# Attention scores from fp32r halves in place of float32 products, and cross-attention queries over 512 columns, in a two-layer decoder

## The chip, the cores and the metric

The kernel runs on one core of a Trainium2 chip. The metric is the device time of one launch, in microseconds (us); less is better. A second record, the trace, holds every instruction of one execution, and the profile is a page made from it. The engines are called PE (TensorE's matmuls), PEld (TensorE's loads of the stationary matrix), DVE (VectorE), ACT (ScalarE), POOL (GpSimd) and SP (the engine whose queue issues the DMAs here).

## The reference

The input x has 16 batches of 64 tokens of width 512, and a context of the same shape. Six blocks follow one another; after each, x becomes the layer norm of x plus the block's output.

```python
x = _layernorm(x + _L0_attn_ref(...))    # causal GQA, 32 query heads, 8 kv heads, width 128
x = _layernorm(x + _L0_xattn_ref(...))   # linear attention over channels, 8 heads of 64
x = _layernorm(x + _L0_ffn_ref(...))     # int4 weights with group scales, inner width 1792
x = _layernorm(x + _L1_attn_ref(...))    # causal GQA with an ALiBi bias on sqrt(distance)
x = _layernorm(x + _L1_xattn_ref(...))   # GQA on the context, queries and keys over their rms
x = _layernorm(x + _L1_ffn_ref(...))     # dense base plus gated low-rank experts
```

The three attentions with 32 heads share one shape: for each batch and kv head, four query heads of 64 queries meet 64 keys.

```python
scores = einsum(q, k) / sqrt(128) + bias     # bias: causal mask, ALiBi, or the given mask
out = softmax(scores) @ v @ w_o
```

All is float32.

## The kernel before

A float32 matrix is used on TensorE as two fp32r matrices: hi, the value rounded to fp32r, and lo, the rest. `mm3` (L101) computes a product as hi*hi + hi*lo + lo*hi, three matmuls into one PSUM bank. `split_sb` and `split_ps` make the halves: ScalarE copies hi, then GpSimd (from SBUF) or VectorE (from PSUM) subtracts. A few small products go to TensorE as plain float32; the trace records each of these as two matmuls. Among them are the scores.

**Tiling.** There are eight token tiles of 128 (two batches each) and two halves of 512 tokens. `Attn` (L737) is one attention layer. For L0 and L1, `q_unit` makes the queries of one query head for half of the tokens, transposed, into `qt` [128, 8 batches, 256], and `k_unit` the keys into `kt`; both copy from a bank of tag `mm` on ScalarE. For the cross attention, `qn_front` (L790) makes the queries of a token tile, token-major, in a bank `fx` as two halves of 256 columns, and divides them by their rms (`rms`); `qn_back` (L803) transposes them into `qt`. The keys of the context are made early by `kv_stream` (L165) and go through DRAM (`ktd`), the values too (`xvd`).

**The stream.** `Stream.run` (L970) goes through steps; a step is four batches of one kv head, and a layer has 32. Within a step, projections for two steps later, the transposes of the probabilities (`pt`, L874), the output projection of the step before (`oproj`, L897), the product with V (`av`, L884) and the scores of two steps later (`scores`, L847) follow one another. `scores` makes eight products of [128 (two heads' queries)] x [64 keys] into the one bank `sc`, then runs the softmax: scale and mask, maximum, subtraction, exponent, sum, division, and the split into `p`, hi and lo side by side.

**What runs beside it.** `fill` puts pieces of other blocks between the parts of a step. Beside the first half of L0's attention runs `k_stream` (L271), the linear attention's key side; beside the second half `q_stream(0)` (L359), its query side in five stages with lags in ticks. Then `l0_ffn` (L440) runs beside `q_stream(1)` and `kv_stream`. L1's attention and the cross attention are one stream, and the last ffn's steps are filled in at its end.

**What sets the order.** The code's order gives priorities; a planner places the instructions on each engine's queue before the run, and may let a ready one pass one that waits for a buffer. Each engine takes its queue in order. Buffers are rings by tag:

```python
BUFS = {"st": 6, "wq": 6, "wo": 6, "wk": 2, "wv": 2, "v": 4, "vs": 4, "qt": 2, "kt": 2, "s": 3, "p": 3, "pts": 2, "ot": 4}
BANKS = {"mm": 2, "fx": 3, "sc": 1, "pt": 1, "o": 1}
```

All eight PSUM banks are used. `fx` serves `k_stream`, `q_stream`, `qn_front`, `qn_back`, and parts of the L0 ffn, whose partial products go through the banks of `PART_BANKS` in turn. `st` holds the loads from DRAM before they are split; `v` holds the halves of V on their way to DRAM (`store_v`, L147).

Of the kernel before, what the change touches and what calls it, by code (L numbers as in the profile page):

```python
# [21 lines left out]
B, S, D = 16, 64, 512          # batches, tokens of a batch, model width  # L22
NT = B * S // 128              # token tiles of 128 (two batches each)
KV, G, HD = 8, 4, 128          # kv heads, query heads of each, head width
FF = 1792 // 128               # tiles of the L0 ffn's inner width
NEG = -1.0e30

# A float32 matrix x is used on the tensor engine as hi + lo, two fp32r
# matrices: hi = x rounded to fp32r, lo = x - hi, which is exact.  A product is
# hi*hi + hi*lo + lo*hi in float32 accumulation.  # L30


# Tiles in SBUF by tag: how many, each of the size of the first use.
BUFS = {"st": 6, "wq": 6, "wo": 6, "wk": 2, "wv": 2, "v": 4, "vs": 4, "qt": 2, "kt": 2, "s": 3, "p": 3, "pts": 2, "ot": 4}
BANKS = {"mm": 2, "fx": 3, "sc": 1, "pt": 1, "o": 1}
# The banks that the partial products of the L0 ffn and its down products go through in turn.
PART_BANKS, DOWN_BANKS = ("o", "sc", "fx", "fx", "fx"), ("o", "sc")
# L0 ffn tiles (14 for each half of the tokens) from this one on go with integer weights.
INT_FROM = 6
# The order in which the L1 ffn's steps of the last four token tiles are taken, by step of the stream and fill point.  # L40
# [7 lines left out]
class Net:  # L48
    def __init__(self, ctx, tc, a):
# [14 lines left out]
        # x by token tile; x transposed, hi and lo, by half of the tokens: [d, dk, token]  # L64
# [9 lines left out]
    def soon(self):  # L74
        """The softmax and what feeds its products goes before the projections' own evacuations."""
        return self.tc.high_priority(offset=100)
# [7 lines left out]
    def split_sb(self, src, hi, lo, fast=False):  # L84
        """hi, lo from float32 in SBUF."""
        self.nc.scalar.copy(hi, src)  # L86
        (self.nc.vector if fast else self.nc.gpsimd).tensor_tensor(lo, src, hi.bitcast(F32), ALU.subtract)  # L87

    def split_ps(self, src, hi, lo):
        """hi, lo from float32 in PSUM."""  # L90
        self.nc.scalar.copy(hi, src)  # L91
        self.nc.vector.tensor_tensor(lo, src, hi.bitcast(F32), ALU.subtract)  # L92

    def load_split(self, src, hi, lo, fast=False):
        """DRAM [128, n <= 1024] -> hi, lo in SBUF."""
# [5 lines left out]
    def mm3(self, out, pairs, first=True, last=True):  # L101
        """out (+)= sum over pairs (lh, ll, rh, rl) of lh*rh + lh*rl + ll*rh."""
# [6 lines left out]
    def rpow(self, out, v, eps, scale=1.0):  # L109
        """out = (v * scale + eps) ** -0.5"""  # L110
# [36 lines left out]
    def store_v(self, vd, t, col, ps):  # L147
        """V [128 tokens, 256] of a token tile -> hi, lo in DRAM, columns col.."""
# [5 lines left out]
    def rms(self, src, dst):  # L154
        """dst [128, n, 128] = src (PSUM) over its rms along the last axis; the last step is returned."""
# [9 lines left out]
    def kv_stream(self):  # L165
        """K (normalized, transposed) and V of the context, to DRAM; a unit of work at a time."""
        nc, a = self.nc, self.a
        self.ktd = self.dram.tile([KV, HD, B * S], F32, name="ktd")
# [12 lines left out]
        def back(hp, t, kn):  # L181
            pk = self.bank("pt")[:, 0:256].rearrange("p (h t) -> p h t", h=2)
            for i in range(2):
                nc.tensor.transpose(pk[:, i], kn[:, i], self.ident)
            ks = self.t("pts", [128, 2, 128])
            nc.scalar.activation(ks, pk, AF.Copy, scale=w)
            nc.sync.dma_start(self.ktd[2 * hp:2 * hp + 2, :, t * 128:(t + 1) * 128].rearrange("h d t -> d h t"), ks)
# [38 lines left out]
    def load_dup(self, src):  # L226
        """src [64, 512] on both halves of the partitions."""
# [5 lines left out]
    def lin_setup(self, ctx):  # L233
# [5 lines left out]
        # WW[c, h, o] = sum over e of Wv[h, e, c] Wout[o, h, e] less its mean over o, on both halves  # L239
# [23 lines left out]
    def half_split(self, src, half):  # L263
        """[64, 512] on the partitions of a half -> hi and lo stacked on 128."""
# [6 lines left out]
    def k_stream(self):  # L271
        """The keys' side: M[b][hd, o] = (softmax(K) V^T Wout^T) / 8, less its mean over o, to DRAM.

        An item is two of the four 128 rows hd of a batch; its four stages are spread over the ticks."""
# [5 lines left out]
        def logits(i):  # L280
# [11 lines left out]
            # exp of the logits [hd, n] less their maximum; the sum divides later  # L292
# [66 lines left out]
    def q_stream(self, half):  # L359
        """The queries' side, the residual, LN and transposition of x; a chunk of 128 n at a time, in stages."""  # L360
# [4 lines left out]
        self.split_sb(self.load_dup(self.a["wq_lin"]), *wq)  # L365

        def logits(c):
# [10 lines left out]
            s = live[c] = self.t(("s", "p")[c % 2], [128, 8, 64])  # L378
# [15 lines left out]
        def transpose(c):  # L394
# [4 lines left out]
            qh = qhs[c] = ex.tile([128, 4, 128], F32, name="le", bufs=3)  # L399
            nc.scalar.copy(flat(qh), pt)  # L400

        def out(c):
# [9 lines left out]
            if u == 1 and k == 3:  # L412
                # over the deviation along o
                z2 = ex.tile([128, 8, 64], F32, name="le", bufs=3)
# [15 lines left out]
        stages = ((5, out), (4, transpose), (2, norm), (1, exp), (0, logits))  # L430
# [9 lines left out]
    def l0_ffn(self, final):  # L440
        """Half after half of the tokens; a unit of work at a time.

        A tile of the inner width is an item.  Either its gate and up weights are multiplied by their scales
        (hi, lo), or the integers go to the tensor engine as they are, which takes two products rather than
        three, and the sum over the groups of a scaled product is left to the vector engine.  An int4 weight is
        exact in fp32r, as is any integer of up to 11 bits: its lo is zero."""
# [4 lines left out]
        def dequant(q, s, hi, lo):  # L451
            """q [128, 1024] ints times s (the same on all partitions) -> hi, lo."""
# [40 lines left out]
        for n, (half, it, ints) in enumerate(items):  # L493
# [3 lines left out]
            if i == 0:  # L497
                pair = self.t("qt", [128, 2, 2, 512], FR)
            # silu(gate) * up, with sigmoid(gate) = (1 + tanh(gate / 2)) / 2
# [27 lines left out]
            self.split_sb(sg, pair[:, 0, i], pair[:, 1, i])  # L527
# [6 lines left out]
            if i == 1:  # L534
                if pend:
                    dn = load_down(g)
                pend = (half, g, dn, pair[:, 0], pair[:, 1])
# [5 lines left out]
    def l1_ffn_setup(self, cp):  # L543
        """The weights; a load at a time."""
# [23 lines left out]
    def l1_ffn(self, t, end):  # L568
        """A token tile: gate, base, experts with residual, LN, out; three steps.  At the end the stream's banks are free."""
# [9 lines left out]
        # threshold: 0.125 / (1 + exp(-(z + b)))  # L579
# [36 lines left out]
    def run(self):  # L616
# [5 lines left out]
        NS = 4 * KV                                  # steps of a layer  # L622
# [11 lines left out]
        with ExitStack() as ctx:  # L634
            # L0: attention; the linear attention's keys beside its first half, its queries a half later
# [460 lines left out]
```

## Time and profile before

| | us |
|---|---|
| three runs | 2274.55, 2277.70, 2279.82 |
| median of the runs | 2277.70 |
| profiled execution, first to last instruction (its span) | 2275.4 |
| PE busy | 2208.5 |
| PEld busy | 1917.7 |
| DVE busy | 1346.0 |
| POOL busy | 1172.9 |
| ACT busy | 1124.1 |

The profiled execution has no other time of its own than the span; the median of the runs is 2.3 us above it. The granted TensorE clock is 0.994 of full speed. The stages by window: L0's attention up to some 690 us, the L0 ffn with the rest of the linear attention and the context's keys and values up to some 1150, L1's attention to some 1700, the cross attention and the last ffn to the end.

A line of the groups by line and shape reads: line, engine, operation, output <- inputs (partitions x elements), count | busy us, mean ns of one | idle time before them. A line of the timeline reads: start, us from the start of the first to the end of the last of the merged instructions, engine, line, operation, tiles, shape, count.

### The profile page before, as it was taken

To read this page: it belongs to the slowest core of one execution; us is meant where nothing else is said; L and a number is where in the kernel's file an instruction comes from. 1 tells how busy PE (TensorE), PEld (TensorE's weight loads), DVE (VectorE), ACT (ScalarE), POOL (GpSimd) and SP (SyncE) were. 2 spreads that over 40 slices of the span, in tenths; PEclk is the share of its full clock that TensorE was granted. 3 is DMA by queue.
4 is the path that set the end of the run, shared out by engine and by line. 5 is a ranking of instruction groups with operands and counts; after the bars stand their busy time and mean duration, and the time that the engine had idled before them with its cause. 6 is when DMAs were issued, how large, how long until landed. Compare 5 with 4: busy or idle time off the path is not lost.

```text
span 2275.4 us, 36680 instructions
## 1 busy us (share of the span) xinstructions
PE 2208.5 (97%) x13200; PEld 1917.7 (84%) x13200; DVE 1346.0 (59%) x2523; ACT 1124.1 (49%) x2195; POOL 1172.9 (52%) x1001
## 2 busy tenths in 40 slices
PE   8999999999999999999999999999999999999998
PEld 7888888888888777777788888888898899988996
DVE  3655555667645789887743343433356566666656
ACT  5665556555444455555444444444444454443442
POOL 3533334455554655464654554545455666554641
PEclk9999999999999999999999999999999999999999
DMA  7533333322334322456543443334333343332320
GB/s 231 158 115 109 112 105 120 110 84 77 91 114 154 120 83 86 153 180 184 156 144 106 131 126 119 116 111 140 107 113 101 115 123 99 103 105 85 112 70 29
DMA packets 255317, 267.24 MB, mean 117 GB/s; under 512 B 32672, under 2 KB 168352, under 8 KB 255136
## 3 DMA queue, kind: packets, MB, share of 16 engines
q1 hardware_dynamic: 255136, 264.90, 38.1%
q8 instruction: 105, 1.72, 0.3%
q14 instruction: 76, 0.62, 0.1%
HBM read 231.26 MB, written 33.55 MB: 116 GB/s over the span
## 4 chain that ended last, share of the span: by engine, by line
PE 79%; DMA 5%; DVE 5%; POOL 5%; issue 2%; ACT 2%; SPq 0%; POOLq 0%; DVEq 0%; ACTq 0%
PE mm L105 16%; PE mm L106 15%; PE mm L107 15%; PE sc L856 6%; PE o L889 4%; PE fx L105 3%; PE fx L107 3%; PE fx L106 3%; PE pt L878 2%; DMA st<-in_down_s 1%; POOL wo L87 1%; PE fx L325 1%; POOL wq L87 1%; PE fx L298 1%; PE fx L316 1%
## 5 line engine op out<-in xcount | busy, mean ns | idle before, releaser
L87 POOL TENSOR_TENSOR wq<-st,wq 128x512 fp32r<-128x512 f32 x200 | 263.7, 1331 | 329.2 <-ACT wq L86 326.1
L107 PE MATMUL mm<-wo,ot 128*128 128x512 f32 x896 | 352.2, 393 | 0.0
L87 POOL TENSOR_TENSOR wo<-st,wo 128x512 fp32r<-128x512 f32 x226 | 296.6, 1342 | 96.8 <-ACT wo L86 88.0
L105 PE MATMUL mm<-wo,ot 128*128 128x512 f32 x768 | 315.2, 410 | 3.4 <-DVE x L904 3.1
L904 DVE TENSOR_TENSOR x<-x,mm 128x512 f32<-128x512 f32 x192 | 131.1, 683 | 308.2 <-PE mm L107 307.8
L106 PE MATMUL mm<-wo,ot 128*128 128x512 f32 x768 | 301.1, 392 | 0.0
L105 PE MATMUL mm<-xth,wq 128*128 128x512 f32 x512 | 204.9, 400 | 0.6 <-DVE v L92 0.3
L106 PE MATMUL mm<-xtl,wq 128*128 128x512 f32 x512 | 200.9, 392 | 0.0
L107 PE MATMUL mm<-xth,wq 128*128 128x512 f32 x512 | 200.6, 392 | 0.0
L107 PEld LDWEIGHTS mm<-wo,ot 128*128 128x128 f32 x896 | 169.3, 189 | 37.1
L91 ACT CAST ot<-o 128x512 fp32r<-128x512 f32 x192 | 112.3, 585 | 174.6 <-PE o L889 173.6
L114 POOL TENSOR_TENSOR r<-e,nhalf 128x4 f32<-128x4 f32 (+1 forms) x96 | 88.6, 923 | 203.2 <-DVE e L113 194.2
L86 ACT CAST wq<-st 128x512 fp32r<-128x512 f32 x204 | 123.8, 620 | 130.7 <-PE mm L106 73.5
L856 PEld LDWEIGHTS sc<-kt,qt 128*128 128x128 f32 x1536 | 184.4, 193 | 3.1
L856 PE MATMUL sc<-kt,qt 128*128 128x64 f32 x1536 | 185.0, 273 | 0.0
L92 DVE TENSOR_TENSOR ot<-o,ot 128x512 fp32r<-128x512 f32 x192 | 132.0, 687 | 81.8 <-ACT ot L91 81.5
L870 POOL TENSOR_TENSOR s<-s,rc 128x512 f32<-128x512 f32 x96 | 100.6, 1048 | 141.7 <-DVE rc L869 77.4
L105 PEld LDWEIGHTS mm<-wo,ot 128*128 128x128 f32 x768 | 144.6, 188 | 27.9 <-DVE x L904 3.4
L106 PEld LDWEIGHTS mm<-wo,ot 128*128 128x128 f32 x768 | 145.3, 189 | 24.1
L86 ACT CAST wo<-st 128x512 fp32r<-128x512 f32 x226 | 129.7, 624 | 41.0 <-PE mm L106 21.9
L105 PE MATMUL fx<-wq,xth 128*128 128x256 f32 x512 | 149.3, 292 | 0.0
L107 PE MATMUL fx<-wq,xtl 128*128 128x256 f32 x512 | 145.5, 284 | 0.0
(283 smaller groups left out, 5626.1 us busy)
## 6 DMA issues: line engine op xcount, KB each, us to landing
st<-in_wq SPq DMA_DIRECT2D x128, 256.0 KB, 3.1
st<-in_wo SPq DMA_DIRECT2D x128, 256.0 KB, 3.1
vs<-v SPq DMA_DIRECT2D x256, 128.0 KB, 3.1
v<-v SPq DMA_DIRECT2D x128, 128.0 KB, 2.7
st<-in_wqx SPq DMA_DIRECT2D x64, 256.0 KB, 2.9
st<-in_wox SPq DMA_DIRECT2D x64, 256.0 KB, 3.4
vs<-xv SPq DMA_DIRECT2D x128, 128.0 KB, 3.0
st<-in_gu_q SPq DMA_DIRECT2D x56, 256.0 KB, 3.0
```

Source lines behind the costliest of these rows:

```text
L86: self.nc.scalar.copy(hi, src)
L87: (self.nc.vector if fast else self.nc.gpsimd).tensor_tensor(lo, src, hi.bitcast(F32), ALU.subtract)
L91: self.nc.scalar.copy(hi, src)
L92: self.nc.vector.tensor_tensor(lo, src, hi.bitcast(F32), ALU.subtract)
L105: self.nc.tensor.matmul(out, lh, rh, start=first and i == 0, stop=False)
L106: self.nc.tensor.matmul(out, lh, rl, start=False, stop=False)
L107: self.nc.tensor.matmul(out, ll, rh, start=False, stop=last and i == n - 1)
L114: self.nc.gpsimd.tensor_tensor(out, e, self.nhalf[:, :n], ALU.pow)
L856: nc.tensor.matmul(sc[:, i * 64:(i + 1) * 64], qt[:, c + b, gp * 128:(gp + 1) * 128], kt[:, (c + b) * 64:(c + b + 1) * 64], start=True, st ...
L870: nc.gpsimd.tensor_tensor(x, x, rc.unsqueeze(2).to_broadcast([128, 8, 64]), ALU.mult)
L889: nc.tensor.matmul(o[:, b * 256:(b + 1) * 256], self.vs[s][i][:, bp * 2 + b], pts[:, b * 256:(b + 1) * 256], start=i == 0, stop=i == 1)
L904: self.nc.vector.tensor_tensor(n.x[t], n.x[t], ps, ALU.add)
```

## The change

The queries and keys of all three attentions are kept as fp32r hi and lo. The keys' halves lie side by side, so that a block of scores is two products: hi of the queries with hi and lo of the keys (128 columns), and lo of the queries with hi of the keys (64 columns, added to the first). The eight blocks of a step now fill two banks, and the softmax's first operation is done in four parts. The evacuations of queries and keys become splits, the context's keys go through DRAM as pairs. Cross queries take their weights by rows of the input instead of by columns, so that a product is 512 columns wide. To make room, `fx` has two banks, several rings are shorter, the query tiles are six small ones, and `q_stream` keeps its intermediate tiles in a ring of its own. All comments are removed, which is left out here.

```diff
-BUFS = {"st": 6, "wq": 6, "wo": 6, "wk": 2, "wv": 2, "v": 4, "vs": 4, "qt": 2, "kt": 2, "s": 3, "p": 3, "pts": 2, "ot": 4}
-BANKS = {"mm": 2, "fx": 3, "sc": 1, "pt": 1, "o": 1}
-PART_BANKS, DOWN_BANKS = ("o", "sc", "fx", "fx", "fx"), ("o", "sc")
+BUFS = {"st": 5, "wq": 6, "wo": 6, "wk": 2, "wv": 2, "v": 2, "vs": 4, "qt": 6, "kt": 2, "s": 3, "p": 2, "pts": 2, "ot": 3}
+BANKS = {"mm": 2, "fx": 2, "sc": 2, "pt": 1, "o": 1}
+PART_BANKS, DOWN_BANKS = ("o", "sc", "sc", "fx", "fx"), ("o", "sc")
...
     def kv_stream(self):
-        self.ktd = self.dram.tile([KV, HD, B * S], F32, name="ktd")
+        self.ktd = self.dram.tile([KV, HD, B, 2 * S], F32, name="ktd")
...
-            ks = self.t("pts", [128, 2, 128])
-            nc.scalar.activation(ks, pk, AF.Copy, scale=w)
-            nc.sync.dma_start(self.ktd[2 * hp:2 * hp + 2, :, t * 128:(t + 1) * 128].rearrange("h d t -> d h t"), ks)
+            ks = self.t("pts", [128, 4, 128], FR)
+            pb = pk.rearrange("p h (b t) -> p (h b) t", b=2)
+            nc.scalar.activation(ks[:, :, 0:64], pb, AF.Copy, scale=w)
+            nc.vector.scalar_tensor_tensor(ks[:, :, 64:128], pb, w, ks[:, :, 0:64].bitcast(F32), ALU.mult, ALU.subtract)
+            for i in range(2):
+                nc.sync.dma_start(self.ktd[2 * hp + i, :, 2 * t:2 * t + 2], ks[:, 2 * i:2 * i + 2].bitcast(F32))
...
     def q_stream(self, half):
+        ring = [ex.tile([128, 2, 512], F32, name="le", bufs=3) for _ in range(3)]
...
-            s = live[c] = self.t(("s", "p")[c % 2], [128, 8, 64])
+            s = live[c] = ring[c // 2 % 2][:, c % 2].rearrange("p (h d) -> p h d", h=8)
...
-            qh = qhs[c] = ex.tile([128, 4, 128], F32, name="le", bufs=3)
+            qh = qhs[c] = ring[2][:, c % 2].rearrange("p (j n) -> p j n", j=4)
...
-                z2 = ex.tile([128, 8, 64], F32, name="le", bufs=3)
+                z2 = self.t("s", [128, 8, 64])
...
-        stages = ((5, out), (4, transpose), (2, norm), (1, exp), (0, logits))
+        stages = ((4, out), (3, transpose), (2, norm), (1, exp), (0, logits))
...
     def l0_ffn(self, final):
-                pair = self.t("qt", [128, 2, 2, 512], FR)
+                pair = [self.t("qt", [128, 2, 512], FR) for _ in range(2)]
...
     def k_unit(self, half, h):
-        kt = self.kt[half, h] = n.t("kt", [128, 512])
+        kt = self.kt[half, h] = n.t("kt", [128, 8, 128], FR)
...
-        self.nc.scalar.copy(kt, ps)
+        n.split_ps(ps.rearrange("p (b t) -> p b t", b=8), kt[:, :, 0:64], kt[:, :, 64:128])
+
+    def q_tiles(self, half, h):
+        self.qt[half, h] = [[self.n.t("qt", [128, 4, 256], FR) for _ in range(2)] for _ in range(2)]
...
     def q_unit(self, half, h, g):
-        self.nc.scalar.copy(self.qt[half, h][:, :, g * 64:(g + 1) * 64], ps.rearrange("p (b q) -> p b q", b=8))
+        for q, qt in enumerate(self.qt[half, h]):
+            n.split_ps(ps[:, q * 256:(q + 1) * 256].rearrange("p (b q) -> p b q", b=4),
+                       *[t[:, :, g * 64:(g + 1) * 64] for t in qt])
...
     def qn_front(self, half, h, i):
-        for gp in range(2):
-            w = self.wqs[h, gp]
-            n.mm3(ps[:, gp * 256:(gp + 1) * 256], [n.xt_slices(t, k) + (w[0][:, k], w[1][:, k]) for k in range(4)])
+        ws = [[flat(w).rearrange("p (k c) -> p k c", k=2) for w in self.wqs[h, kp]] for kp in range(2)]
+        n.mm3(ps, [n.xt_slices(t, k) + (ws[k // 2][0][:, k % 2], ws[k // 2][1][:, k % 2]) for k in range(4)])
...
     def qn_back(self, half, h, i):
-        dst = self.qt[half, h][:, 2 * i:2 * i + 2].rearrange("p b (g q) -> p b g q", g=4)
-        self.nc.scalar.copy(dst, ps.rearrange("p g (b q) -> p b g q", b=2))
+        r = slice(2 * (i % 2), 2 * (i % 2) + 2)
+        n.split_ps(ps.rearrange("p g (b q) -> p b g q", b=2),
+                   *[t[:, r].rearrange("p b (g q) -> p b g q", g=4) for t in self.qt[half, h][i // 2]])
...
     def scores(self, s):
-        qt, kt, c = at.qt[half, h], at.kt[half, h], (s % 2) * 4
-        sc = n.bank("sc")
-        for b in range(4):
-            for gp in range(2):
-                i = b * 2 + gp
-                nc.tensor.matmul(sc[:, i * 64:(i + 1) * 64], qt[:, c + b, gp * 128:(gp + 1) * 128],
-                                 kt[:, (c + b) * 64:(c + b + 1) * 64], start=True, stop=True)
-        m, d = (at.mask, (8, 64)) if at.alibi is None else (at.alibi[:, h], (4, 128))
+        (qh, ql), kt, c = at.qt[half, h][s % 2], at.kt[half, h], (s % 2) * 4
+        sc = [n.bank("sc").rearrange("p (u i k) -> p u i k", u=2, i=4) for _ in range(2)]
+        for i in range(8):
+            o, b, q = sc[i // 4][:, :, i % 4], i // 2, slice((i % 2) * 128, (i % 2) * 128 + 128)
+            nc.tensor.matmul(o, qh[:, b, q], kt[:, c + b].rearrange("p (u k) -> p u k", u=2), start=True, stop=False)
+            nc.tensor.matmul(o[:, 0], ql[:, b, q], kt[:, c + b, 0:64], start=False, stop=True)
+        m, d = (at.mask, (4, 64)) if at.alibi is None else (at.alibi[:, h], (2, 128))
...
-            nc.vector.scalar_tensor_tensor(flat(x).rearrange("p (a b) -> p a b", b=d[1]),
-                                           sc.rearrange("p (a b) -> p a b", b=d[1]), 1.0 / math.sqrt(HD),
-                                           m.unsqueeze(1).to_broadcast([128, d[0], d[1]]), ALU.mult, ALU.add)
+            for hf in range(2):
+                xv = flat(x[:, hf * 4:hf * 4 + 4])
+                hh, hl = [flat(sc[hf][:, u]) for u in range(2)]
+                nc.vector.scalar_tensor_tensor(xv.rearrange("p (a b) -> p a b", b=d[1]),
+                                               hh.rearrange("p (a b) -> p a b", b=d[1]), 1.0 / math.sqrt(HD),
+                                               m.unsqueeze(1).to_broadcast([128, d[0], d[1]]), ALU.mult, ALU.add)
+                nc.vector.scalar_tensor_tensor(xv, hl, 1.0 / math.sqrt(HD), xv, ALU.mult, ALU.add)
...
 def _arrange(i):
+    r["wqx"] = inout(i["L1_xattn_q_proj_w"].T, KV).reshape(KV, 128, 2, 1024).transpose(0, 2, 1, 3)
```

## The prediction

> **What bounds the kernel now.** I read the page's first part and its chain of waits, then the table of windows, the groups by line and shape, and last the timeline.
>
> ```profile
> PE 2208.5 (97%) x13200; PEld 1917.7 (84%) x13200; DVE 1346.0 (59%) x2523; ACT 1124.1 (49%) x2195; POOL 1172.9 (52%) x1001
> PE 79%; DMA 5%; DVE 5%; POOL 5%; issue 2%; ACT 2%; SPq 0%; POOLq 0%; DVEq 0%; ACTq 0%
> ```
>
> TensorE is busy 2208.5 of 2275.4 us; all its idle time is 67 us. The execution's span stands 2.3 us under the median of the three runs, 2277.7; I sum against the span and add 2.3 at the end. The measurement can tell about 0.2% (4.6 us) from no change.
>
> ```profile
> 171.00:228.00 57.00, 57.00 (x352) 50.50 (x351) 31.92 (x64) 32.18 (x69) 21.28 (x18) 1.00 0.36 110
> 513.00:570.00 57.00, 56.63 (x363) 48.73 (x362) 44.43 (x92) 31.23 (x56) 31.26 (x28) 1.00 0.26 77
> 855.00:912.00 57.00, 52.30 (x294) 41.51 (x293) 51.00 (x109) 30.52 (x57) 32.38 (x28) 1.00 0.29 89
> 1900.00:2000.00 100.00, 97.82 (x682) 90.25 (x682) 64.52 (x114) 45.47 (x88) 61.69 (x53) 0.98 0.35 106
> ```
>
> Columns: window, length, then busy time of PE, PEld, DVE, ACT, POOL. In the attention of L0 and L1 TensorE has no gap. Only where VectorE reaches 51 of 57 us (L0's ffn beside the second queries' stream) is TensorE held up, 4.7 us in 57. So a saving in TensorE's work counts almost whole, and what the change lays on VectorE is free only while its chains stay short enough for the PSUM banks.
>
> **What a product costs.** Busy times of matmuls overlap, so the price is the distance from start to start.
>
> ```profile
> 1834.52 1.90 PE L856 MATMUL sc<-kt,qt 128*128 128x64 f32 x16
> 1836.43 0.28 PE L106 MATMUL fx<-wq,xth 128*128 128x256 f32 x1
> 1836.54 0.28 PE L107 MATMUL fx<-wq,xtl 128*128 128x256 f32 x1
> 1839.06 0.28 PE L107 MATMUL fx<-wq,xtl 128*128 128x256 f32 x1
> 1839.18 0.45 PE L878 MATMUL pt<-identr,p 128*128 128x128 f32 x4
> 1841.64 0.39 PE L105 MATMUL mm<-wo,ot 128*128 128x512 f32 x1
> 1841.87 0.39 PE L106 MATMUL mm<-wo,ot 128*128 128x512 f32 x1
> ```
>
> A step's eight score products are sixteen records, two each: (1.90 - 0.27)/15 = 0.108 us apart, 1.73 us a step, 166 us in the 96 steps. An fp32r product of 256 columns takes (1839.06 - 1836.54)/21 = 0.120 us, one of 512 takes 0.23 (0.227 in long rows). Four fp32r transposes of 128 columns are (0.45 - 0.24)/3 = 0.07 apart.
>
> ```profile
> L856 PE MATMUL sc<-kt,qt 128*128 128x64 f32 x1536 | 185.0, 273 | 0.0
> L856 PEld LDWEIGHTS sc<-kt,qt 128*128 128x128 f32 x1536 | 184.4, 193 | 3.1
> L106 PEld LDWEIGHTS fx<-wq,xth 128*128 128x128 f32 x512 | 98.6, 193 | 0.1
> L878 PEld LDWEIGHTS pt<-identr,p 128*128 128x128 f32 x768 | 84.4, 141 | 19.7 <-POOL p L87 5.3
> L92 DVE TENSOR_TENSOR v<-mm,v 128x256 fp32r<-128x256 f32 x96 | 40.0, 417 | 32.3 <-ACT v L91 29.3 <-DMA vs<-v 1.7
> L91 ACT CAST v<-mm 128x256 fp32r<-128x256 f32 x96 | 35.5, 370 | 70.7 <-PE mm L107 63.0 <-DMA v<-v 5.5 <-DMA st<-in_ctx 2.1
> L861 DVE SCALAR_TENSOR_TENSOR s<-sc,xmask 128x512 f32<-128x512 f32 x32 | 22.0, 686 | 7.4 <-PE sc L856 7.4
> ```
>
> **Scores on TensorE: nothing gained.** Before, eight products are 16 loads and 16 records. After, eight blocks have a product of 128 columns and one of 64, each with its own stationary matrix: again 16 loads and 16 records. What sets the 0.108? The f32 products of 128 columns at L336 (shown below, four records in 0.61 us) are (0.61 - 0.275)/3 = 0.112 apart: double the columns, the same distance, so the load and not the columns is paid. An fp32r load of a product lasts 193 ns, like the f32 one; only transposes load in 141. So I take 16 x 0.108 = 1.73 us, no difference. The trace has no fp32r product narrower than 256 columns, so both ends stay open. Below: the transposes' 0.07 for all 16 gives 1.12, -0.61 x 96 = -59 us. Above: a narrow product as dear as the next wider row of the same kind, 0.227 for 128 and 0.120 for 64 columns, gives 8 x 0.347 = 2.78, +1.05 x 96 = +101 us. I stay at zero because the load row is the nearer.
>
> The Trainium skill (TensorE: Matmul & The Clock Gate, LDWEIGHTS) puts a load at its columns over 1.2 GHz, 107 ns for 128, and this speaks against the change; the trace's 0.108 agrees. [...]
>
> **Cross queries.** Each of the 64 units (16 heads and halves, four token tiles) replaces 24 products of 256 columns by 12 of 512: 24 x 0.120 = 2.88 against 12 x 0.227 = 2.72, so -0.16 x 64 = -10 us. TensorE has little idle time in this stage (2.2 of 100 us), so it counts whole.
>
> **VectorE and ScalarE.** Every evacuation that was one copy becomes a split. Queries of L0 and L1: 128 units x 2 x 0.417 = 107 us of new VectorE work; keys 32 x 0.687 = 22; cross queries 64 x 0.687 = 44 (0.687 is the split of 512 columns into ot); context keys 32 x 0.417 = 13. The softmax's first operation becomes four on 256 columns, 4 x 0.417 - 0.69 = 0.98 more, 94 us in all. Together 280 us: VectorE goes from 1346 to 1626. ScalarE gets 128 x (2 x 0.370 - 0.584) = 20 us. A head of L0 takes on 3.3 + 0.7 + 2.0 = 6 us: in the window at 513, where a step takes some 29 us, VectorE rises from 44 to 50 of 57, the level at which TensorE loses 4.7 us further on. In L1's attention VectorE has room (about 40%); in the cross attention it goes from 64 to some 78 of 100. The longer softmax lies under the two steps that separate scores from their use and costs nothing there; without that cover it would be 0.98 x 96 = 94 us.
>
> **The banks.** The second score bank comes from fx, which goes from three to two. Three streams use fx: the linear attention's keys, its queries, and the cross queries. In the keys' stream:
>
> ```profile
> 398.18 1.03 PE L316 MATMUL fx<-ident,le 128*128 128x128 f32 x8
> 399.05 0.61 PE L336 MATMUL fx<-ww,lkx 128*128 128x128 f32 x4
> 399.48 0.69 DVE L92 TENSOR_TENSOR le<-fx,le 128x512 fp32r<-128x512 f32 x1
> ```
>
> The eight transposes fill two banks; L336 follows in a third. With two, it must wait till VectorE has split the first, 399.48 + 0.69 = 400.17: 1.12 us. I made the same subtraction for all groups that use fx (when the bank used two groups earlier is released, less when the group starts now): 64 us in the keys' stream, 125 in the queries' streams, 28 at the first ffn tiles, 15 in the cross attention: 231 us if every matmul kept its place. (L0 ffn partial products are left out: they keep five banks and use fx less.) The order need not stay: at 1448.98 the transposes of L878 ran ahead of a projection that the code writes before them, while that waited for its bank. So the bounds are 0 and 231; I take a fifth, 46 us, since independent projections of 2.7 us are usually at hand to cover a wait of 1 to 2.
>
> **Buffers and DMAs.** V's tiles go from four to two, so a V unit waits until the store before it has landed (2.8 us after issue); behind that wait stand ScalarE's queue and a bank of mm. V units are a step (16 to 29 us) apart, except in the few back to back before each stream's first step and in the context stream, some 9 us apart, whose stores queue on SP behind loads. Staging tiles go from six to five, while SP waits long for POOL to free them. Bounds 0 and 3 us x 44 units (12 back to back, 32 of the context) = 130; I take 5, as the 9 us of the many are three times a landing. The transposed keys' DMAs double in bytes and 32 stores more are issued on SP, some 0.35 us each beside its other issues: nothing. The query buffers become six quarter-size tiles: at the first write for a new head four are taken, two of them last read by scores one step earlier; nothing. p, ot, and the queries' ring are last read before their next writer, and the queries' last stage, moved a tick earlier, issues the same four products: nothing.
>
> **Sum.** 2275.4 - 10 + 0 + 46 + 5 = 2316.4 on the span; with 2.3 around it 2319 us.
>
> **The rivals.**
> Dear narrow products: the +101 of above, less a fifth of the waits, since slower TensorE gives VectorE time: 2319 + 92 = 2411; half of the price, 2365. For it: all fp32r products of before are 256 wide or more, even where 137 columns would do (L572). Against: the equal loads.
> Cheap loads: the -59 of above, 2319 - 59 = 2260. For it: L878's 0.07. Against: its loads are shorter, 141 ns, than any product's.
> Faster through cover: the waits on fx are all passed over by other matmuls, as three banks left almost none. Place: order of TensorE in L0. Price: 46 + 5 fall to some 3, 2271. It decides for faster once the waits stay under 10 - 4.6 = 5 us. For it: 57 of 57 us in L0's attention now. Against: VectorE at 50 of 57, where the ffn stage shows 4.7 us lost per window.
> VectorE as the bound: if all L0 attention beside the queries' stream (some 230 us) lost as the ffn stage does, 4 x 4.7 = 19 us more, 2338: inside my own case.
>
> **How the numbers follow.** My case 0.50, 2285 to 2350. Dear narrow products 0.23, cheap loads 0.13, cover 0.14. The range 2250 to 2405 leaves out the dear end of the first rival (0.1) and the low end of the second (0.07). Faster: most of cheap loads and of cover, 0.25; within 0.2%: 0.07; slower 0.68.
>
> **What would show it.** Right: 1536 score records at about 0.11 us, the cross units in 2.7 us, PE waits at fx for VectorE from 60 to 690 us, VectorE near 1626. Wrong: score steps near 1.1 or 2.8 us, or PE idle no more than now.

## The result, and the profile after

The kernel after takes 2478.2 us (median; 2477.0 to 2481.8), the one before 2278.8 beside it: 1.0879 times as long, interval 1.0859 to 1.0899. The forecast was 2319, range 2250 to 2405: the direction was right and the size wrong by 159 us. The profiled execution's span is 2480.0 us, so 204.6 more than before's 2275.4, at a granted clock of 0.971 (before 0.994).

The page's first part, and the row of the chain of waits:

```profile
PE 2283.0 (92%) x12432; PEld 1910.8 (77%) x12432; DVE 1595.2 (64%) x3195; ACT 1147.2 (46%) x2323; POOL 1161.8 (47%) x1001
...
PE 3%; DVE 1%; POOL 0%; issue 0%; ACT 0%; POOLq 0%; ACTq 0%
```

TensorE is idle for 2480.0 - 2283.0 = 197 us, before 67: +130 of the 204.6. The other 74.5 are longer busy time. A granted clock of 0.971 is an estimated (1 - 0.971) x 2480.0 = 72 us lost, if TensorE is at work throughout; before it is 14. So some 58 of the 74.5 are a slower clock. The chain is followed back over 4% of the span alone, and says nothing of the stages.

Windows of after (columns as in the prediction: window, length, busy of PE, PEld, DVE, ACT, POOL; behind them the clock, the DMA share and GB/s):

```profile
171.00:228.00 57.00, 52.83 (x310) 44.94 (x309) 34.26 (x73) 30.85 (x68) 19.18 (x16) 0.97 0.33 98
...
930.00:987.00 57.00, 50.80 (x260) 40.23 (x259) 47.90 (x103) 27.24 (x50) 24.30 (x24) 0.92 0.17 51
1425.00:1539.00 114.00, 106.88 (x591) 90.96 (x590) 53.50 (x106) 48.41 (x100) 50.34 (x41) 0.99 0.35 109
...
2040.00:2140.00 100.00, 88.77 (x490) 74.66 (x489) 65.85 (x117) 42.53 (x79) 52.64 (x45) 0.98 0.31 98
```

The four windows lie in L0's attention, L0's ffn, L1's attention and the cross attention. The gaps are in every stage now, in L1's attention too, where VectorE works 53.5 of 114 us and GpSimd no more. No other engine is busy throughout.

The scores, in the groups by line and shape and in a stretch of the timeline:

```profile
L867 PE MATMUL sc<-kt,qt 128*128 128x128 f32 x768 | 175.8, 299 | 0.0
L868 PE MATMUL sc<-kt,qt 128*128 128x64 f32 x768 | 174.2, 246 | 0.0
...
L868 PEld LDWEIGHTS sc<-kt,qt 128*128 128x128 f32 x768 | 148.0, 193 | 2.3
```

```profile
1487.41 0.31 PE L867 MATMUL sc<-kt,qt 128*128 128x128 f32 x1
1487.55 0.25 PE L868 MATMUL sc<-kt,qt 128*128 128x64 f32 x1
1487.63 0.30 PE L867 MATMUL sc<-kt,qt 128*128 128x128 f32 x1
1487.78 0.25 PE L868 MATMUL sc<-kt,qt 128*128 128x64 f32 x1
1487.86 0.31 PE L867 MATMUL sc<-kt,qt 128*128 128x128 f32 x1
```

A block, two products, takes (1487.86 - 1487.41)/2 = 0.225 us; before it was two records at 0.112 (the prediction's 0.108 is the mean of a row whose first distance is 0.058). TensorE's price of the scores has not changed. TensorE's waits, summed by what released it, the largest of before and then the largest of after:

```profile
PE o L889 <- ACT pts L881: 6.1, 5, 2.5
```

```profile
PE o L904 <- ACT pts L896: 32.5, 25, 4.3
PE fx L105 <- DVE s L162: 22.0, 18, 1.6
PE fx L340 <- DVE le L92: 21.2, 14, 2.8
PE mm L105 <- DVE qt L92: 9.7, 7, 1.6
```

(Total us, times, longest.) The waits at `fx` that the prediction named are there. Above them stands one that it did not name: the product with V (`av`) waits for ScalarE's copy of the transposed probabilities, `pts`.

### The profile page after: what moved, and what is told of

It reads as the page before. It is cut to its first block, busy times and chain, and to the rows that moved or that the text cites. A ratio compares the mean times of both kernels' runs of the same rounds, so it can differ in the third digit from the quotient of the medians.

```text
span 2480.0 us, 36161 instructions
## 1 busy us (share of the span) xinstructions
PE 2283.0 (92%) x12432; PEld 1910.8 (77%) x12432; DVE 1595.2 (64%) x3195; ACT 1147.2 (46%) x2323; POOL 1161.8 (47%) x1001
## 5 line engine op out<-in xcount | busy, mean ns | idle before, releaser
L87 POOL TENSOR_TENSOR wo<-st,wo 128x512 fp32r<-128x512 f32 x226 | 290.3, 1311 | 103.0 <-ACT wo L86 96.5
L92 DVE TENSOR_TENSOR qt<-mm,qt 128x256 fp32r<-128x256 f32 x256 | 108.1, 422 | 239.6 <-ACT qt L91 236.5
L105 PE MATMUL mm<-xth,wq 128*128 128x512 f32 x512 | 212.1, 414 | 13.0 <-DVE qt L92 8.6
L107 PE MATMUL mm<-xth,wq 128*128 128x512 f32 x512 | 205.7, 402 | 0.0
L867 PE MATMUL sc<-kt,qt 128*128 128x128 f32 x768 | 175.8, 299 | 0.0
L868 PE MATMUL sc<-kt,qt 128*128 128x64 f32 x768 | 174.2, 246 | 0.0
L904 PEld LDWEIGHTS o<-pts,vs 128*128 128x128 f32 x768 | 115.3, 191 | 70.3 <-ACT pts L896 55.8
L904 PE MATMUL o<-pts,vs 128*128 128x256 f32 x768 | 127.9, 289 | 43.0 <-ACT pts L896 32.5
```

The source lines that it names most:

```text
L105: self.nc.tensor.matmul(out, lh, rh, start=first and i == 0, stop=False)
L107: self.nc.tensor.matmul(out, ll, rh, start=False, stop=last and i == n - 1)
L867: nc.tensor.matmul(o, qh[:, b, q], kt[:, c + b].rearrange("p (u k) -> p u k", u=2), start=True, stop=False)
L868: nc.tensor.matmul(o[:, 0], ql[:, b, q], kt[:, c + b, 0:64], start=False, stop=True)
L904: nc.tensor.matmul(o[:, b * 256:(b + 1) * 256], self.vs[s][i][:, bp * 2 + b], pts[:, b * 256:(b + 1) * 256], start=i == 0, stop=i == 1)
```

## The experiments

Stages are compared by TensorE's score products: each stage runs from the start of one step's scores to that of another, the same steps in each kernel. L0 is L0's attention from its third step on, X the cross attention. What is lost ahead of the third step (12 us in after) and behind the last scores stands in no column. Time lost against before, in us of the profiled executions:

| | L0 | ffn | L1 | X |
|---|---|---|---|---|
| after | +59.0 | +35.4 | +41.7 | +56.5 |
| a_f32w | +38.8 | +25.0 | +4.2 | +4.7 |
| a_order5 | +42.2 | +28.6 | +3.3 | +8.1 |
| f_order5 | +62.4 | +31.7 | +42.2 | +54.2 |
| a_order (ScalarE) | +46.0 | +28.6 | +6.4 | +59.8 |
| a_orderP (TensorE) | +59.9 | +27.7 | +38.4 | +35.1 |
| a_orderPA (both) | +47.6 | +31.9 | +5.1 | +25.0 |
| a_late | +59.4 | +31.2 | +22.0 | +60.0 |
| b_early | +0.4 | +4.8 | +20.5 | +28.0 |

**The parts, each alone on the kernel before.** The kernel b_fx2 has two banks for `fx` and two for `sc`:

```diff
-BANKS = {"mm": 2, "fx": 3, "sc": 1, "pt": 1, "o": 1}
+BANKS = {"mm": 2, "fx": 2, "sc": 2, "pt": 1, "o": 1}
-PART_BANKS, DOWN_BANKS = ("o", "sc", "fx", "fx", "fx"), ("o", "sc")
+PART_BANKS, DOWN_BANKS = ("o", "sc", "sc", "fx", "fx"), ("o", "sc")
```

> The kernel before with the banks of the changed one alone: fx two, sc two, partial products over o, sc, sc, fx, fx. Theory of the banks: most of the 38 us lost in the linear attention's keys, of the 21 beside its queries and of the 35 in the L0 ffn come back, with the gaps before L336, so 2350 to 2380 us. Theory of the buffers (staging and V tiles): under 15 us, 2280 to 2293. Theory of the added VectorE work: also under 15 us, as the chains are as short as before. All three expect nothing in L1's attention, which does not use fx.

Measured 2305.1, ratio 1.0112 (1.0087 to 1.0137): some +26, between the ranges expected. The profiled execution has +31, of which 22 are in L0's ffn and 11 in L0's attention. The prediction had 46.

The shorter rings (`st` 5, `v` 2, `ot` 3):

> The kernel before with the shorter rings alone: st 5, v 2, ot 3. Theory of the buffers: ScalarE waits for loads as in the changed kernel (88 us for st<-in_wq against 25), its queue is late with the copies of pt, and L1 and the cross attention lose 30 to 60 us, so 2310 to 2340. Theories of the banks and of the VectorE work: within 10 us of before.

Measured 2317.2, 1.0163 (1.014 to 1.0186): +37, where the prediction had 5.

The added work of VectorE: a second pass over every evacuation of queries and keys (here a maximum with itself, which changes nothing), and the softmax's first operation in four parts.

```diff
-        self.nc.scalar.copy(kt, ps)
+        self.nc.scalar.copy(kt, ps)
+        self.nc.vector.tensor_tensor(kt, ps, kt, ALU.max)
...
+            for i in range(4):
+                c = slice(i // 2 * 256, i // 2 * 256 + 256)
+                nc.vector.scalar_tensor_tensor(flat(x)[:, c]..., sc[:, c]..., ALU.mult, ALU.add)
```

> The kernel before with the added evacuation work alone: the queries and keys are copied as in the changed kernel (two copies of 256 columns for the queries), and VectorE then passes over the same values once more (a maximum of a value with itself); the softmax's first operation is four operations on 256 columns, of which two write again what stands there. Banks, rings and products as before. Theory of the VectorE work: VectorE comes to 1626 us, mm banks are released later, and L1 loses some 30 of its 42 us, the whole 60 to 120, 2340 to 2400. Theories of banks and buffers: under 20 us, 2280 to 2298.

Measured 2343.8, 1.0272 (1.0244 to 1.03): +62, in the expected range; but L1 lost 10 us, not 30. Of the two, the softmax alone:

> The kernel before with the softmax's first operation alone in four parts of 256 columns (two of them write again what stands there): 94 us more on VectorE. If its length lies under the two steps between scores and their use, as the prediction has it, within 6 us of before; if the chain to the probabilities is late, a good part of the 64 us of the added work together, 2300 to 2330.

Measured 2318.3, 1.0175 (1.0155 to 1.0195): +40, of which 29.7 in X. TensorE's largest wait there is not at the scores' banks but at the bank `o`, which VectorE's split into `ot` has to empty (15.1 of these 17.2 us are in X):

```profile
PE o L891 <- DVE ot L92: 17.2, 9, 2.6
```

But VectorE is not at work while TensorE waits. One of these waits, in the timeline:

```profile
1946.83 0.58 ACT L91 CAST ot<-o 128x512 fp32r<-128x512 f32 x1
1948.77 0.69 DVE L162 TENSOR_TENSOR s<-fx,r 128x512 f32<-128x512 f32 x1 [3.80 <-POOL r L114]
1949.38 0.68 DVE L92 TENSOR_TENSOR ot<-o,ot 128x512 fp32r<-128x512 f32 x1
1950.21 0.72 PE L891 MATMUL o<-pts,vs 128*128 128x256 f32 x4 [2.04 <-DVE ot L92]
```

The split into `ot` could start at 1947.41, when ScalarE's cast ends. Ahead of it on VectorE's queue stands the norm of a later unit's queries, which waits for GpSimd's `r`, and VectorE is idle for 3.80 us. In X, 9 of the 64 splits stand right behind such a wait of over 1 us, in before none, in after none. So the largest wait that b_soft adds comes from the order of VectorE's queue, not from the length of the softmax.

The cross queries over 512 columns:

> The kernel before with the cross queries' products over 512 columns alone. By the prediction's term, 64 units x (24 x 0.120 - 12 x 0.227) = 10 us less: 2265 to 2273. If the unit's distances are set by something else, no difference.

Measured 2267.7, ratio 0.9957 (0.9944 to 0.997), span 2265.7: 9.7 us less, the prediction's 10.

**All parts together, without the pair.** b_all is before with the banks, the rings, the added work and the wide cross queries, and scores still in float32. a_f32w is after with one float32 product of 128 columns in the pair's place; it leaves out the queries' lo times the keys' hi.

```diff
-            nc.tensor.matmul(o, qh[:, b, q], kt[:, c + b].rearrange(...), start=True, stop=False)
-            nc.tensor.matmul(o[:, 0], ql[:, b, q], kt[:, c + b, 0:64], start=False, stop=True)
+            nc.tensor.matmul(o, qh[:, b, q].bitcast(F32), kt[:, c + b].bitcast(F32).rearrange(...), start=True, stop=True)
```

> The kernel before with banks, shorter rings, added evacuation work and cross queries of 512 columns together, the scores still float32 products. If the fp32r products themselves cost nothing, as the start-to-start distances say (0.143 + 0.080 against 2 x 0.112), this is the changed kernel but for its query ring and tiles: 2450 to 2480 us. If something in the pair form itself costs time, 2400 or less.

> The changed kernel with each block's pair of fp32r products replaced by one float32 product of the queries' hi with hi and lo of the keys, 128 columns (the product with the queries' lo is left out). On TensorE the price is the same: two records 0.112 us apart against 0.143 + 0.080. Rings, tiles, banks, splits and the softmax stay. Theory of the rings and tiles: 2465 to 2490, as changed. Theory of the pair form (it is the fp32r pair, or the order that the planner makes around it, that costs the 110 us which banks, buffers and evacuation work together did not bring): 2350 to 2400.

b_all: 2367.6, 1.0389 (1.0362 to 1.0416). a_f32w: 2364.0, 1.0391 (1.037 to 1.0413). The parts sum to some 26 + 37 + 62 - 10 = 115 and give 89 together; the other 110 us of the change vanish when the pair is one product, though its records take TensorE as long (0.112 us apart in the trace, 0.224 a block; their row is below). a_f32w has after's small query tiles, its ring for the queries' stream and its two `p` tiles, b_all has not; the two take the same time, so together these show no cost.

```profile
L867 PE MATMUL sc<-kt,qt 128*128 128x128 f32 x1536 | 192.9, 276 | 0.5 <-ACT qt L91 0.5
```

**Three products of 64 columns into one bank**, with three banks `fx` and the softmax's first operation in one part, else as after:

> The changed kernel with the scores as three fp32r products of 64 columns into one bank (hi hi, hi lo, lo hi), so that fx has three banks again, sc one, and the softmax one operation. 24 loads instead of 16 cost 8 x 0.112 x 96 = 86 us on TensorE. Theory of the banks and VectorE: these give back 25 + some 30, so 2500 to 2515. Theory of the pair form or the planner: half as many again of the narrow products, 2550 or more.

Measured 2453.2, 1.0773 (1.0749 to 1.0798); both theories had expected 2500 or more. The 64-column records start 0.112 apart too, each with its load of 193 ns, so a step has 24 of them: 24 x 0.112 = 2.69 us against 1.79, 0.9 x 96 = 86 us of TensorE's time. A product of 64 columns takes as long here as a float32 record of 128; this fits a pace set by the loads, which are alike. That the kernel is still 25 us faster than after shows that what it gives back, banks, softmax or queue order, is worth some 111 if the 86 count whole; which of them was not taken apart.

**The order on ScalarE.** In the trace ScalarE takes the same instructions in another order in after than in a_f32w. In L1's attention the cast that splits a later step's probabilities (`p<-s`) stands ahead of the copy `pts<-pt` in 17 of 30 steps of after, in 7 of before, in none of a_f32w; the first `pts` of a step starts there on average 2.17, 0.63 and 0.66 us after its transposes end. One such place in after's timeline:

```profile
1528.61 0.45 PE L893 MATMUL pt<-identr,p 128*128 128x128 f32 x4
...
1530.28 0.62 ACT L86 CAST wq<-st 128x512 fp32r<-128x512 f32 x1 [2.10 <-DMA st<-in_wq]
...
1533.30 0.62 ACT L86 CAST p<-s 128x512 fp32r<-128x512 f32 x1 [1.10 <-POOL s L885]
1533.82 0.58 ACT L896 CAST pts<-pt 128x512 fp32r<-128x512 f32 x1
...
1534.45 0.74 PE L904 MATMUL o<-pts,vs 128*128 128x256 f32 x4 [2.60 <-DMA st<-in_wo]
```

The transposes end at 1529.06. ScalarE stands 2.10 us before a weight cast whose load has not come, then 1.10 us before a cast whose softmax is not done, and the ready copy waits behind both. TensorE loses 2.60 us (the releaser named is not the cause: `pts` is the last thing that `av` needs). The same step where the queues have a_f32w's order (a_order5, below):

```profile
1481.60 0.46 PE L897 MATMUL pt<-identr,p 128*128 128x128 f32 x4
...
1482.18 0.62 ACT L86 CAST wq<-st 128x512 fp32r<-128x512 f32 x1 [0.99 <-DMA st<-in_wq]
...
1483.18 0.59 ACT L900 CAST pts<-pt 128x512 fp32r<-128x512 f32 x1
...
1484.02 0.62 ACT L86 CAST wq<-st 128x512 fp32r<-128x512 f32 x1 [0.25 <-DMA st<-in_wq]
...
1484.72 0.64 PE L908 MATMUL o<-pts,vs 128*128 128x256 f32 x4
...
1485.21 0.62 ACT L86 CAST p<-s 128x512 fp32r<-128x512 f32 x1 [0.57 <-POOL s L889]
```

`pts` starts 1.1 us after its transposes end, the second weight cast and the cast to `p` come behind it, and `av` follows without a gap.

a_late moves that one cast in after; b_early forces the bad order on before:

```diff
+    def finish(self, s, after=None):              # a_late: the split of p, traced after pt(s - 1, 0)
...
+            with n.tc.issue_after(after.ins):     # after: the copy pts
+                n.split_sb(x, p[:, :, 0:64], p[:, :, 64:128])
...
+        if bp == 0 and s and s + 1 in self.p:     # b_early, in pt
+            with n.soon(), n.tc.issue_after(self.cast.ins):
+                nc.scalar.copy(pts, pt.bitcast(F32))
```

> The kernel after, with one move: ScalarE's cast of a step's probabilities (p from s) is queued behind the copy pts from pt that the next product with V waits for. No work is added or removed. Theory (the pair form loses its time because ScalarE's queue has that cast, which waits for the softmax of a later step, before the copy that TensorE needs now): most of the 35 us that L1's attention lost against before come back, and some of the cross attention's 56, so 2400 to 2445 us, ratio to before 1.053 to 1.073, and in L1 the mean delay of the first pts copy falls from 2.2 to about 0.7 us. Rival (the pair form loses its time on TensorE or in VectorE's longer chain, and ScalarE's order only follows from that): 2465 to 2490, ratio 1.081 to 1.093, with the waits moved to another tile.

> The kernel before, float32 scores and all its buffers, with one move: ScalarE's copy pts from pt for the first half of a step is queued behind the cast of the probabilities of the next step (p from s), as the kernel after mostly has it. No work is added. Theory (this order on ScalarE costs TensorE gaps, whatever the form of the scores): L1's attention and the cross attention lose 15 to 40 us each, L0's attention some 10, in all 2300 to 2350 us, ratio 1.01 to 1.03. Rival (the order alone is harmless; it hurts only with a pair of products): within 10 us of before.

a_late: 2458.4, 1.077 (1.0749 to 1.079), between the two expectations. L1 has 20 of its 42 us back and X nothing, so this one cast is half of L1's loss and no more. b_early: 2337.1, 1.0248 (1.0233 to 1.0264), in the range of the theory: with no work added and float32 scores, two instructions exchanged in each step, and the rest planned around that, cost 57 us. L0, where 10 had been expected, lost 0.4, though its `pts` start late as well (2.4 us after the transposes, in before 0.7). The wait is after's:

```profile
PE o L894 <- ACT pts L883: 45.7, 46, 2.9
```

**The two halves of the rings.** 

> The kernel before with five staging tiles instead of six, nothing else. The three shortened rings together cost 37 us, mostly in L0's ffn (14 us), before the first step (9) and in the cross attention (7). Theory A (staging: loads start later, and the casts behind them hold up ScalarE's queue): 2300 to 2315, ratio 1.010 to 1.016. Theory B (the stores of V, which hold their tiles until they have landed): within 8 us of before.

> The kernel before with two tiles for V on its way to DRAM instead of four, and three of the output's instead of four; six staging tiles. Theory A (staging is what costs): within 8 us of before. Theory B (V's tiles, held until the stores land): 2300 to 2315, ratio 1.010 to 1.016, with the loss where V units stand back to back (before the first step) and beside the context's keys and values (L0's ffn).

b_st5: 2311.4, 1.0138 (1.0123 to 1.0153), +31. b_v2, which has the third `ot` tile too: 2290.1, 1.0048 (1.0032 to 1.0063), +11. The staging ring is the dear one: one tile less of six, 19 us in L0's ffn and 9 in X. b_v2 loses 9 ahead of the third step's scores, where V's units stand back to back.

**Form and order exchanged.** The order of each queue is planned before the run, so it can be taken from one kernel and forced on another. The kernel is traced once with one form, the order of its queues is noted, and the other form is traced with an edge of issue order between neighbours of each queue:

```diff
+    _, order = _program(arrays, False)         # a_order5: planned with a_f32w's one product
+    nc, _ = _program(arrays, True, order)      # run: the pair, queued so
...
+        for e in order or ():                  # PE, Activation, DVE, Pool, SP
+            for a, b in zip(order[e], order[e][1:]):
+                tc.add_manual_dep(traced[e][b], net.second.get(traced[e][a].name, traced[e][a].name), ...)
```

> The kernel after, pair of products and all, but with the instructions of every engine queued in the order that the planner made for a_f32w (each pair stands where a_f32w has its one product). Theory (the pair itself costs nothing; what costs is the order of the queues that the planner makes for it): within 15 us of a_f32w's 2364, so 2350 to 2380, with the granted clock back near 0.99. Rival (the pair costs on the chip, on TensorE or by the waits of VectorE for its end): 2440 to 2490. In between, both have a share, in the proportion of the time.

> The reverse: a_f32w's one float32 product a block (the queries' lo is left out of the scores), with every engine's queue in the order that the planner made for the pair of the kernel after. Theory (order): near the kernel after, 2440 to 2490. Rival (the pair on the chip): near a_f32w, 2350 to 2380.

| ratio to before | order planned for the pair | order planned for one product |
|---|---|---|
| the pair | after 1.0879 (1.0859 to 1.0899) | a_order5 1.0390 (1.0372 to 1.0407) |
| one float32 product | f_order5 1.0846 (1.0814 to 1.0878) | a_f32w 1.0391 (1.0370 to 1.0413) |

The traces show the same operations on the same tiles in the same order, on each of the four compute engines, in a_order5 as in a_f32w, and in f_order5 as in after. The columns differ by 4.6 to 4.9 points, 104 to 111 us; the rows by 0.3 points at most, no more than the intervals allow. The pair itself costs nothing on the chip that these runs can tell. TensorE's first waits in a_order5 are those of the banks alone, in f_order5 `pts` is back at the head:

```profile
PE fx L105 <- DVE s L162: 14.6, 21, 1.9
PE fx L302 <- ACT lkx L331: 10.8, 16, 1.2
```

```profile
PE o L908 <- ACT pts L900: 39.7, 26, 4.3
```

a_order5's idle time is 2371.5 - 2235.9 = 136 us and its clock 0.986, 33 us lost; after has 197 and 72. The two differences, 61 and 39, make 100 of the 108.5 us between the spans.

**Whose order.** The same with ScalarE's queue alone (a_order), TensorE's alone (a_orderP), and both (a_orderPA). The queues that are not forced are planned anew around these, so their order changes too:

> The kernel after with ScalarE's queue alone in the order made for a_f32w; the others are planned around it. If ScalarE's order carries the loss: 2355 to 2400. If it is the order of TensorE or VectorE: 2430 to 2490.

> The kernel after with TensorE's queue alone in the order made for a_f32w. If TensorE's order carries the cross attention's loss and ScalarE's that of L1: the cross attention gets some 40 of 56 us back and L1 none, 2430 to 2450. If VectorE's order or the DMAs' carries it: 2465 to 2490. If TensorE's order draws ScalarE's with it, as the planner places both together: 2365 to 2400.

> The kernel after with TensorE's and ScalarE's queues in the order made for a_f32w, VectorE's, GpSimd's and the DMAs' planned around them. If these two carry the loss: 2360 to 2385, as a_order5 (2369). If VectorE's order or the DMAs' carries the cross attention's share: 2415 to 2435, as a_order (2428).

a_order 2427.5, 1.0639 (1.062 to 1.0658); a_orderP 2452.3, 1.074 (1.0709 to 1.0771); a_orderPA 2402.0, 1.0529 (1.0509 to 1.0548). Each fell between the ranges expected of it. Of what a_order5 gives back, ScalarE's queue by itself gives back nearly all in L1, most in L0, and nothing in X. There TensorE's gives back 21 us, both 31, and all five 48: the rest is with VectorE's, GpSimd's and the DMAs' order.

**A faster version.** The wide cross queries on before, and a_late's move with them:

> The kernel before with the cross queries over 512 columns (2267.7 alone) and the cast of the probabilities queued behind the copy that the next product with V waits for, as in a_late. In before that cast stands first in 31 of 92 steps, so if each costs TensorE some tenths of a us there, 2250 to 2266; if it costs only where TensorE is already short of work, 2264 to 2272; if the later split makes the transposes of the next step wait, above 2275.

2265.7, 0.994 (0.9923 to 0.9956); b_c512 has 0.9957 (0.9944 to 0.997). Both beat before and after. The time lies in two of the expected ranges, and the late cast on top can't be told from none.

## Why the prediction was wrong, step by step

**Scores flat on TensorE: right.** 0.225 us a block against 0.224, and the load's 193 ns stayed. Both rivals on the price of narrow products fall: in the pair the 128-column product is followed after 0.143 us, the 64-column one after 0.080, and neither end of the bounds was met. The Trainium skill (TensorE: Matmul & The Clock Gate, Back-to-back issue gap) has the spacing in a stream of loads and products set by both, and gives some 81 ns for a product of 128 columns; the trace's pair takes 0.225 us for two products, 0.112 each, and the measurement decides.

**Cross queries: right.** b_c512 measured 9.7 us less, the term was 10.

**The banks: mechanism right, 46 against 26 alone.** In b_fx2's profiled execution 11 us are lost in L0's attention and 22 in the ffn's stage, where the second queries' stream goes through these banks, and with it the ffn's own partial products, which the term left out; X gained 3. In after itself TensorE's waits at `fx` come to 77 us, in before to 21: the 56 more are near the term of 46. But 21 of them are in X, where the term took at most 15 and where b_fx2 waits no more than before, so there the banks alone do not make the wait. The rival "faster through cover" fails here too.

**"The longer softmax ... costs nothing there": wrong as measured.** b_soft took 40 us more. The two steps may well cover the chain from the scores to `p`: the largest new wait, 15.1 us in X, comes from splits that are queued behind a norm for which VectorE stands idle. What the longer work costs in an unchanged order no run shows. The prediction gave the price without cover, 94, and kept it out of range and rivals. VectorE itself was sized well: 1626 forecast, 1595 measured.

**"Buffers: I take 5": wrong.** 37 measured together; alone the one staging tile, which the term hardly priced, costs 31, and V's tiles, which it looked at, 11 with the third `ot`.

**The step that failed most: each term was worked out in before's queue order.** The fx waits were computed "if every matmul kept its place", and the freedom of the order was counted only in the change's favour. With the pair the five queues stand differently, and that alone is 104 to 111 of the 199 us; the form's own cost can't be told from nothing. The view that could have warned was the waits of `av` for `pts` in before, 6.1 us, with casts that wait for the softmax's result or for a load in the same queue:

```profile
ACT p L86 <- POOL s L870: 98.1, 85, 2.4
ACT wq L86 <- DMA st<-in_wq: 24.9, 21, 3.1
```

**The clock was left out.** By the estimate above, some 58 of the 204.6 us are half speed. A stretch of 3.41 us at half speed costs a TensorE that is at work 1.7, so a gap of some 2 us that brings one costs nearly twice its length; each wait of the sum was priced at its length alone.

**Not settled.** What about the pair makes the planner order the queues otherwise was not tried. The parts (banks, rings, softmax) were each run as planned for themselves, so their costs, too, are resource and order in one, and the share of each is open. That they sum to 115 and give 89 together shows that they overlap, not where.

## What to carry to other kernels

Where a planner fixes the queues, a change of one instruction's form changes all of them; before believing that an operation is dear, force the other kernel's order on it and the other way round. Look first at ready evacuations that stand behind casts which wait for a load or a chain. And count a gap of some 2 us or more on a nearly gapless TensorE at its own length plus the 1.7 us that the clock took here.

## What the runs showed of the hardware

In after, half speed came after short gaps. A stretch of after's cross attention, in the timeline and the windows:

```profile
2004.60 0.39 PE L107 MATMUL mm<-wo,ot 128*128 128x512 f32 x1
2007.49 0.84 PE L904 MATMUL o<-pts,vs 128*128 128x256 f32 x4 [2.50 <-ACT pts L896]
2008.13 0.63 PE L105 MATMUL fx<-wq,xth 128*128 128x512 f32 x1
2008.56 0.63 PE L106 MATMUL fx<-wq,xth 128*128 128x512 f32 x1
```

```profile
2007.96:2011.37 3.41, 3.41 (x11) 2.73 (x10) 2.26 (x5) 1.10 (x2) 2.93 (x3) 0.50 0.02 8
2011.37:2014.78 3.41, 3.41 (x18) 2.81 (x18) 1.14 (x3) 1.08 (x2) 0.58 (x1) 1.00 0.00 0
```

A gap of 2.50 us, then 3.41 us at a clock of 0.50, in which products of 512 columns start 0.43 apart in place of 0.23. All half-speed stretches of after are 3.41 us long or twice that, but for the one cut off by the end. From 1680 us on there are fourteen; thirteen follow a gap of 1.38 to 4.31 us, the last comes when TensorE's work is over. They all lie on one grid of 3.413 us. Take after's cells of this grid that ran at full clock, but the first. Where TensorE was idle for over 1.84 us of a cell, half speed always followed, 25 times; between 1.2 and 1.84 us it did in 12 of 40; under 1.2 never, in 618. That is after's trace alone: in b_soft a cell with 1.91 us idle was not followed by half speed. Nor is a gap always needed. Before has a stretch of 6.83 us at half speed from 54.39 on without any gap ahead of it; sixteen products of 64x64 (L248, `fx<-st`) run there, and no run takes this apart.

The Trainium skill (TensorE: Matmul & The Clock Gate, Part 1) has a free-running window of 3413 ns and a clock of half or full: the trace agrees, with its 3.41 us and 0.50. The same page (HAM oscillation) gives as its rule no idle gaps over some 3.4 us; here gaps of 1.38 to 2.8 us were enough, and the measurement decides.
